# Making the attention's products on GpSimd, in chunks of 1024 elements

## The chip, the cores and the metric

The kernel runs on one core of a Trainium2 chip. The core has a matrix engine (TensorE, PE in the profile), a vector engine (VectorE, DVE), a scalar engine (ScalarE, ACT), a general engine (GpSimd, POOL) and a queue for transfers (SyncE, SP). Each engine carries out its own instructions in their order, and waits on semaphores for what other engines made. The metric is the device time of one launch in microseconds. The kernel before took 472.21 us, the median of three runs (471.46 to 473.74).

## The reference

The input x has shape (2, 1024, 256), in float32. Two branches work on the normalized x, and both results are added to x.

```
xn = layernorm(x)
out = x + attention(xn) + experts(xn)

attention: each row of 256 is 16 tokens of 16 numbers
  qkv = tok @ qkv_w                      # q, k, v of 16 each
  two branches of 8 channels; in each, windows of 8 tokens
    s = softmax(q k^T / sqrt(8))         # 8 x 8 in every window
    o = s @ v + depthwise 3x3 convolution of v
  tok + layernorm(concat(o) @ proj_w + proj_b) * ln_w + ln_b

experts: 16 experts of 176 hidden units, gated by a sigmoid router
  the two best of four groups, then the six best experts of a row
  sum of weight * (silu(x @ gate^T) * (x @ up^T)) @ down^T
  and one shared expert of twice that width, for every row
```

In the attention each window has 8 queries, 8 keys and 8 channels. The scores of a window are 512 products, summed by eights. The weighted values are another 512 products, also summed by eights.

## The kernel before, in words

The work starts with loading x, normalizing it and transposing it (`xnT`). The router's choice follows on VectorE, with the shared expert's products beside it on TensorE. The rows are then sorted so that rows with the same set of experts come together. From about 100 us on, the experts' products run over 16 tiles of 128 sorted rows.

The loop at L965 writes the main part in program order. One *unit* is two expert products: `up` (L823) makes gate and up products on TensorE (L827), ScalarE takes the silu (L829), and VectorE multiplies the two and the row's weight into `hms` (L830). One unit later `hidden` transposes that (L841, L843), and another unit later `finished` makes the down products (L853 for two experts of one tile, L861 for extras) and adds them up (L908, or L916 for extras). Sixteen tiles have three units each. 13 units of *extras*, for rows whose tile has more than six experts, come after the first four tiles. When a tile is complete, `added` (L920) issues an indirect transfer from GpSimd's queue that adds its rows to the output (L922). The first four tiles' additions wait for the extras. `sorted_tile` (L796) gathers a tile's rows with an indirect transfer from GpSimd's queue (L798), transposes them on TensorE (L802), and prepares the weights on VectorE (L805, L807, L809, L810).

Between the units the loop lays steps of the attention. Every step has a cost, and a step is laid whenever the costs so far fall behind the share of the units that are done. A planner then orders each engine's instructions by its own estimate of when they can start; the order within an engine can differ from the program's.

The attention runs over four pairs of image b and half h, called heads in this document. For each, `gather` copies the rows, `project` (L654) makes q, k and v with eight products on TensorE (L656) and copies them on ScalarE (L658 to L661) into `qk` and `v`. Then 16 positions of windows, n = 0 to 15, are worked through, NW = 4 at a time, so that one chunk is 4 x 8 x 8 x 8 = 2048 elements in each of 128 partitions:

- `products` (L665) multiplies q and k of the chunk, each broadcast (L669), and `scores` sums the last axis (L673). Both are VectorE's.
- `highest` takes the maximum (L679), subtracts it (L680), and ScalarE takes the exponential (L681).
- `weighted` (L687) multiplies s and v (L690), and `values` sums (L695). `totals` makes the denominators (L684, L685) after the first weighted chunk.
- `divide` (L703) multiplies by the reciprocals, and `transposed` turns the result on TensorE (L710) and copies it to `oT` (L712).

The chunk's products lie in a work tile with the tag "prod", of which there is one buffer; later the first of the two result tiles `att` takes the same tag. `qk` and `v` have one buffer each, so the next head's projections wait for the last products of this head.

After the fourth head, `attended` (L746) runs eight times: the output projection and the convolution on TensorE (L761), the second normalization on ScalarE and VectorE (L771 to L783). `attention_added` (L945) adds the result to the output with transfers from GpSimd's queue (L946).

Of the kernel before, what the change touches and what calls it, by code (L numbers as in the profile page):

```python
# [8 lines left out]
F32 = mybir.dt.float32  # L9
# [4 lines left out]
ALU = mybir.AluOpType  # L14
# [8 lines left out]
P = 128  # L23
B, H, W = 2, 1024, 256
C = 16
HD = 8
WIN = 8
NW = 4
E, I = 16, 176
LAST = I - P  # L30
HALF = P // 2
# [18 lines left out]
def csw_block_moe(ctx: ExitStack, tc: tile.TileContext, x, qkv_w, conv_w0, conv_b0, conv_w1, conv_b1,  # L50
# [19 lines left out]
    nc = tc.nc  # L70
# [3 lines left out]
    work = ctx.enter_context(tc.tile_pool(name="work", bufs=1))  # L74
# [69 lines left out]
    for c in range(16):  # L144
        n = sum(P // 2 if k % 2 == 0 else P for k in range(c)) + (((16 - c) * P - 1) / 2 if c % 2 == 0 else 0)
# [186 lines left out]
    full = [P, 16, E]  # L332
# [114 lines left out]
    for c in range(15, -1, -1):  # L447
        n = 16 - c
# [186 lines left out]

    oT = big.tile([P, 4, 2, 4, P], F32, name="oT", tag="oT")

    def attention(b, h):
        steps = []

        qk = work.tile([P, 2, 2, 8, WIN, HD], F32, tag="qk", name=f"qk{b}{h}")
        v = work.tile([P, 2, 8, HD, WIN], F32, tag="v", name=f"v{b}{h}")
        s = work.tile([P, 16, WIN, WIN], F32, tag="f1024", name=f"s{b}{h}", bufs=3)
        o = work.tile([P, 16, WIN, HD], F32, tag="f1024", name=f"o{b}{h}", bufs=3)
        sums = small.tile([P, 16, WIN], F32, name=f"sums{b}{h}", tag="sums")
        rows = work.tile([P, 8, P], F32, tag="f1024", name=f"rows{b}{h}", bufs=3)
        full = [P, NW, WIN, WIN, HD]

        def gather():
            for i in range(2):  # L650
                nc.scalar.copy(rows[:, 4 * i : 4 * i + 4].rearrange("p i (w r) -> p i w r", r=4),
                               xnT[:, h, :, 64 * b : 64 * b + 64].rearrange("p (i r) (w u) -> p u i w r", r=4, u=2)[:, i])

        def project(i):  # L654
            pq = ps_m.tile([P, 3, 8, C], F32, tag="m", name="pq")
            nc.tensor.matmul(pq.rearrange("p s t c -> p (s t c)"), lhsT=rows[:, i],  # L656
                             rhs=wq.rearrange("p s t c -> p (s t c)"), start=True, stop=True)
            nc.scalar.copy(qk[:, :, 0, i], pq[:, 0:2, :, 0:HD])  # L658
            nc.scalar.copy(qk[:, :, 1, :, i], pq[:, 0:2, :, HD:C])
            nc.scalar.copy(v[:, 0, i], pq[:, 2, :, 0:HD].rearrange("p t c -> p c t"))  # L660
            nc.scalar.copy(v[:, 1, :, :, i], pq[:, 2, :, HD:C])  # L661

        held = {}

        def products(n):  # L665
            pr = work.tile([P, NW, WIN, WIN, HD], F32, tag="prod", name="pr")
            br, m = n // 8, n % 8
            q_, k_ = (qk[:, part, br, m : m + NW] for part in range(2))
            nc.vector.tensor_tensor(pr, q_.unsqueeze(3).to_broadcast(full), k_.unsqueeze(2).to_broadcast(full), ALU.mult)  # L669
            held[n] = pr  # L670

        def scores(n):
            nc.vector.tensor_reduce(out=s[:, n : n + NW], in_=held.pop(n), axis=AX.X, op=ALU.add)  # L673

        rows_s = s.rearrange("p n q k -> p (n q) k")

        def highest():
            top = small.tile([P, P], F32, tag="top", name="top", bufs=1)
            nc.vector.tensor_reduce(out=top, in_=rows_s, axis=AX.X, op=ALU.max)  # L679
            nc.vector.tensor_tensor(rows_s, rows_s, top.unsqueeze(2).to_broadcast([P, P, WIN]), ALU.subtract)  # L680
            nc.scalar.activation(rows_s, rows_s, AF.Exp, scale=HD**-0.5)  # L681

        def totals():
            nc.vector.tensor_reduce(out=sums.rearrange("p n q -> p (n q)"), in_=rows_s, axis=AX.X, op=ALU.add)  # L684
            nc.vector.reciprocal(sums, sums)  # L685

        def weighted(n):  # L687
            pr = work.tile([P, NW, WIN, HD, WIN], F32, tag="prod", name="pv")
            br, m = n // 8, n % 8
            nc.vector.tensor_tensor(pr, s[:, n : n + NW].unsqueeze(3).to_broadcast(full),  # L690
                                    v[:, br, m : m + NW].unsqueeze(2).to_broadcast(full), ALU.mult)
            held[n] = pr

        def values(n):
            nc.vector.tensor_reduce(out=o[:, n : n + NW], in_=held.pop(n), axis=AX.X, op=ALU.add)  # L695

        def divide():
            xo = held["xo"] = work.tile([P, 8, 8, C], F32, tag="xo", name=f"xo{b}{h}")
            for br in range(2):
                to = xo[:, :, :, HD * br : HD * br + HD]  # L700
                if br:
                    to = to.rearrange("p i t c -> p t i c")
                nc.vector.tensor_tensor(to, o[:, 8 * br : 8 * br + 8],  # L703
                                        sums[:, 8 * br : 8 * br + 8, :].unsqueeze(3).to_broadcast([P, 8, WIN, HD]),
                                        ALU.mult)

        def transposed(i):
            po = ps_m.tile([P, 4, P], F32, tag="m", name="po")
            for j in range(4):
                nc.tensor.transpose(po[:, j, :], held["xo"][:, i + j].rearrange("p t c -> p (t c)"), ident)  # L710
            to = oT.rearrange("p g h r (b w i) -> p g h b i w r", b=B, i=2)[:, :, h, b, i // 4]
            nc.scalar.copy(to, po.rearrange("p j (w r) -> p j w r", r=4))  # L712


        steps.append((512, gather))
        for i in range(8):
            steps.append((512, lambda i=i: project(i)))
        for n in range(0, 16, NW):
            steps.append((2048, lambda n=n: products(n)))
            steps.append((2048, lambda n=n: scores(n)))  # L720
        steps.append((2048, highest))
        for n in range(0, 16, NW):
            steps.append((2048, lambda n=n: weighted(n)))
            if n == 0:
                steps.append((2048, totals))
            steps.append((2048, lambda n=n: values(n)))
        steps.append((1024, divide))
        for i in (0, 4):
            steps.append((512, lambda i=i: transposed(i)))
        return steps  # L730

    def edges():

        xe = [work.tile([P, 2, 4, P], F32, tag=tag, name="xe") for tag in ("v", "xo")]
        for t in xe:
            nc.gpsimd.memset(t, 0.0)
        pairs = xnT.rearrange("p h l (q e) -> p l h q e", e=2)
        for h in range(2):  # L740
            above, below = (t[:, h].rearrange("p l (q e) -> p l q e", e=2) for t in xe)
            nc.vector.tensor_copy(above[:, :, :, 1], pairs[:, 12:16, h, :, 0])
            nc.vector.tensor_copy(below[:, :, :, 0], pairs[:, 0:4, h, :, 1])
        return xe
# [181 lines left out]
    att = []  # L926

    def all_steps():
        for steps in (extras_listed(), weights_prepared()):
            for _ in steps:  # L930
                yield 1024, lambda: None
        yield from attention_steps()

    def attention_steps():
        for b in range(B):
            for h in range(2):
                yield from attention(b, h)
        xe = []
        yield 1024, lambda: xe.extend(edges())
        att.extend(work.tile([P, 8, W], F32, tag=tag, name="att") for tag in ("prod", "qk"))  # L940
        for g in range(4):
            for h in range(2):
                yield 3584, lambda: attended(g, h, xe, att)
# [122 lines left out]
```

## Time and profile before

| | |
|---|---|
| median of three runs | 472.21 us |
| the profiled execution | 474.59 us |
| its span | 472.9 us |
| TensorE busy | 414.2 us |
| VectorE busy | 324.6 us |
| ScalarE busy | 213.1 us |
| GpSimd busy | 72.7 us |
| VectorE in products (L669, L690) | 36.6 + 36.6 us |
| VectorE in sums (L673, L695) | 36.5 + 36.4 us |
| mean granted TensorE clock | 0.978 |

A row of a group gives the line, the engine, the operation, the output and input with partitions x elements, and the count; behind the first bar the busy time in us and the mean of one in ns; behind the second the engine's idle time before these instructions and what ended it. A row in order of time starts with the start and the duration in us; a bracket at its end gives the idle time before it and what ended that. "PEld" is TensorE loading weights, beside its products. TensorE's busy time is modelled at the ends and overlaps from one product to the next, so that a busy TensorE is not one at its peak.

### The profile page before, as it was taken

How to read it: one execution, taken by the hardware profiler on the slowest of the kernel's cores; microseconds unless marked ns; L12 is line 12 of the kernel's file. 1: busy time of each engine (PE TensorE's matmuls, PEld its weight loads, DVE VectorE, ACT ScalarE, POOL GpSimd, SP SyncE). 2: the span in 40 equal slices, each digit the busy share in tenths (PEclk: the TensorE clock that was granted, in tenths of full speed). 3: DMA queues.
4: the chain of work that ended last, by engine and by line, in shares of the span. 5: the costliest groups of instructions: out<-in, count | busy, mean ns of one | idle time of the engine just before them, and what ended most of it. 6: DMA issues, size and time to landing. Idle time of an engine off the chain costs nothing.

```text
span 472.9 us, 6428 instructions
## 1 busy us (share of the span) xinstructions
PE 414.2 (88%) x1726; PEld 258.7 (55%) x1727; DVE 324.6 (69%) x587; ACT 213.1 (45%) x510; POOL 72.7 (15%) x94
## 2 busy tenths in 40 slices
PE   0999999997989789999999998889989998999950
PEld 0446566464557566655566665546655555557740
DVE  4525956745789994997972799969999456665210
ACT  1946167222644537546425536263422566674210
POOL 6300000425530000000002301201111101002321
PEclk9999999997999999999999999999999999999995
DMA  8999950423120000000012211101231112104841
GB/s 225 325 291 272 285 163 2 101 47 79 57 58 28 21 21 19 22 19 28 24 30 42 43 36 36 35 16 31 44 71 30 14 54 67 54 14 74 124 77 15
DMA packets 37714, 35.39 MB, mean 75 GB/s; under 512 B 4000, under 2 KB 36112, under 8 KB 37648
## 3 DMA queue, kind: packets, MB, share of 16 engines
q1 hardware_dynamic: 30448, 25.37, 19.3%
q0 software_dynamic: 6176, 8.56, 11.6%
q10 hardware_dynamic: 1056, 1.05, 0.7%
q8 instruction: 16, 0.26, 0.2%
q14 instruction: 18, 0.15, 0.1%
HBM read 26.45 MB, written 10.62 MB: 78 GB/s over the span
## 4 chain that ended last, share of the span: by engine, by line
DVE 36%; PE 33%; DMA 13%; ACT 7%; issue 6%; POOL 1%; DVEq 1%; POOLq 0%; SPq 0%; ACTq 0%
PE pr_u L827 8%; DVE pv L690 6%; DVE o L695 6%; DVE s L673 5%; DVE pr L669 5%; DMA xg<-xw_d,of 5%; PE pp L761 4%; DVE hms L830 4%; DMA out_dram<-att 3%; PE pr_y L861 3%; PE pg L266 3%; DMA out_dram<-ysum,of 3%; PE py L281 2%; PE pq L656 2%; DMA xx<-in_x_dram 2%
## 5 line engine op out<-in xcount | busy, mean ns | idle before, releaser
L827 PE MATMUL pr_u<-w1s,xsT 128*128 x384 | 129.8, 469 | 5.2 <-DVE hms L830 5.0
L829 ACT ACTIVATE sg<-pr_u 128x176 f32<-128x176 f32 x122 | 38.3, 317 | 128.7 <-PE pr_u L827 98.2
L827 PEld LDWEIGHTS pr_u<-w1s,xsT 128*128 128x128 f32 x384 | 70.8, 191 | 42.5 <-DVE hms L830 10.5
L922 POOL DMA_INDIRECT out_dram<-ysum,of x16 | 27.0, 1691 | 246.8 <-DVE ysum L916 116.6
L830 DVE SCALAR_TENSOR_TENSOR hms<-sg,w,pr_u 128x176 f32<-128x176 f32 x96 | 36.9, 390 | 38.0 <-ACT sg L829 37.9
L669 DVE TENSOR_TENSOR pr<-qk 128x2048 f32<-128x2048 f32 x16 | 36.6, 2287 | 7.8 <-ACT qk L658 7.6
L841 PE MATMUL ph<-ident,hms 128*128 128x128 f32 x183 | 33.3, 279 | 6.9 <-DVE hms L830 5.4
L690 DVE TENSOR_TENSOR pv<-s,v 128x2048 f32<-128x2048 f32 x16 | 36.6, 2286 | 3.5 <-ACT s L681 3.5
L841 PEld LDWEIGHTS ph<-ident,hms 128*128 128x128 f32 x183 | 23.4, 142 | 26.3 <-DVE hms L830 11.3
L673 DVE TENSOR_REDUCE s<-pr 128x256 f32<-128x2048 f32 x16 | 36.5, 2279 | 0.0
L695 DVE TENSOR_REDUCE o<-pv 128x256 f32<-128x2048 f32 x16 | 36.4, 2272 | 0.0
L827 PE MATMUL pr_u<-w1s,xd 128*128 x104 | 33.5, 460 | 1.1 <-ACT xd L868 1.1
L843 ACT COPY hT<-ph 128x384 f32<-128x384 f32 x61 | 29.1, 478 | 3.3 <-PE ph L841 1.7
L853 PE MATMUL pr_y<-w2a,hT 128*128 x96 | 28.7, 381 | 0.0
L853 PE MATMUL pr_y<-w2b,hT 112*128 x96 | 28.7, 379 | 0.0
L853 PE MATMUL pr_y<-wts,hT 128*128 128x256 f32 x96 | 28.6, 379 | 0.0
L656 PE MATMUL pq<-wq,rows 128*128 128x384 f32 x64 | 25.0, 501 | 2.3 <-ACT oT L712 1.7
L827 PEld LDWEIGHTS pr_u<-w1s,xd 128*128 128x128 f32 x104 | 19.7, 190 | 11.0 <-ACT xd L868 1.5
L281 PE MATMUL py<-room 128*128 128x256 f32 x96 | 23.9, 387 | 1.4 <-DVE room L275 1.4
L266 PE MATMUL pg<-xnT,room 128*128 128x512 f32 x48 | 24.1, 614 | 0.0
L798 POOL DMA_INDIRECT xg<-xw_d,of x16 | 20.2, 1262 | 22.4 <-PE px__928 L802 8.6
L266 PE MATMUL pu<-xnT,room 128*128 128x512 f32 x48 | 23.0, 602 | 0.0
(314 smaller groups left out, 623.4 us busy)
## 6 DMA issues: line engine op xcount, KB each, us to landing
w1s<-in_w_dram SPq DMA_DIRECT2D x22, 256.0 KB, 5.5
wts<-in_w_dram SPq DMA_DIRECT2D x61, 64.0 KB, 2.1
wts<-in_w_dram SPq DMA_DIRECT2D x61, 48.0 KB, 1.7
xw_d<-xx SPq DMA_DIRECT2D x4, 544.0 KB, 8.2
w2a<-in_w_dram SPq DMA_DIRECT2D x4, 512.0 KB, 11.5
out_dram<-ysh POOLq DMA_DIRECT2D x4, 512.0 KB, 5.5
xr<-xw_d SPq DMA_DIRECT2D x4, 512.0 KB, 3.8
out_dram<-att POOLq DMA_DIRECT2D x4, 512.0 KB, 7.2
```

What stands on the lines that cost most here:

```text
L266: nc.tensor.matmul(ps, lhsT=w1h[:, half, h, P * m : P * m + P], rhs=xnT[:, h, 4 * k : 4 * k + 4, :].rearrange("p l q -> p (l q)"), start=( ...
L281: nc.tensor.matmul(py, lhsT=hms[k, m][:, P * c : P * c + P], rhs=w2h[:, m], start=(m == 0), stop=(m == 2))
L656: nc.tensor.matmul(pq.rearrange("p s t c -> p (s t c)"), lhsT=rows[:, i], rhs=wq.rearrange("p s t c -> p (s t c)"), start=True, stop=True)
L669: nc.vector.tensor_tensor(pr, q_.unsqueeze(3).to_broadcast(full), k_.unsqueeze(2).to_broadcast(full), ALU.mult)
L673: nc.vector.tensor_reduce(out=s[:, n : n + NW], in_=held.pop(n), axis=AX.X, op=ALU.add)
L690: nc.vector.tensor_tensor(pr, s[:, n : n + NW].unsqueeze(3).to_broadcast(full), v[:, br, m : m + NW].unsqueeze(2).to_broadcast(full), ALU. ...
L695: nc.vector.tensor_reduce(out=o[:, n : n + NW], in_=held.pop(n), axis=AX.X, op=ALU.add)
L827: nc.tensor.matmul(pu, lhsT=lhs[:, h, :], rhs=w1s[:, :, h, bass.ds(e * I, I)], start=(h == 0), stop=(h == 1))
L829: nc.scalar.activation(sg, pu[:, 0, :], AF.Silu)
L830: nc.vector.scalar_tensor_tensor(hm[:, 0:I], sg, w, pu[:, 1, :], op0=ALU.mult, op1=ALU.mult)
L841: nc.tensor.transpose(ph[:, s, :], units[:, P * s : P * s + P], ident)
L853: nc.tensor.matmul(py, lhsT=l_, rhs=r_, start=start and n == 0, stop=stop and n == 2)
```

## The change

A chunk has two positions (1024 elements) instead of four. The product tile is made once, with room for two chunks, and chunks take the halves in turn; all four heads and the later `att` tile use it. The products are issued on GpSimd instead of VectorE, with the same operands. The sums stay on VectorE. The steps are laid so that a product comes one chunk ahead of the sum: product 0, product 1, sum 0, product 2, sum 1, and so on. The denominators (`totals`) come before the first weighted chunk instead of after it. A step of a product or sum costs 1024 instead of 2048, so a head's steps cost the same in all.

```diff
-NW = 4
+NW = 2
...
+    prods_ = []
+
     def attention(b, h):
         steps = []
+        if not prods_:
+            prods_.append(work.tile([P, 2, NW, WIN, WIN, HD], F32, tag="prod", name="prods"))
+        prods = prods_[0]
...
         def products(n):
-            pr = work.tile([P, NW, WIN, WIN, HD], F32, tag="prod", name="pr")
+            pr = prods[:, n // NW % 2]
             br, m = n // 8, n % 8
             q_, k_ = (qk[:, part, br, m : m + NW] for part in range(2))
-            nc.vector.tensor_tensor(pr, q_.unsqueeze(3).to_broadcast(full), k_.unsqueeze(2).to_broadcast(full), ALU.mult)
+            nc.gpsimd.tensor_tensor(pr, q_.unsqueeze(3).to_broadcast(full), k_.unsqueeze(2).to_broadcast(full), ALU.mult)
             held[n] = pr
...
         def weighted(n):
-            pr = work.tile([P, NW, WIN, HD, WIN], F32, tag="prod", name="pv")
+            pr = prods[:, n // NW % 2]
             br, m = n // 8, n % 8
-            nc.vector.tensor_tensor(pr, s[:, n : n + NW].unsqueeze(3).to_broadcast(full),
+            nc.gpsimd.tensor_tensor(pr, s[:, n : n + NW].unsqueeze(3).to_broadcast(full),
                                     v[:, br, m : m + NW].unsqueeze(2).to_broadcast(full), ALU.mult)
...
-        for n in range(0, 16, NW):
-            steps.append((2048, lambda n=n: products(n)))
-            steps.append((2048, lambda n=n: scores(n)))
+        def in_turn(product, total):
+
+            for n in range(0, 16 + NW, NW):
+                if n < 16:
+                    steps.append((1024, lambda n=n: product(n)))
+                if n >= NW:
+                    steps.append((1024, lambda n=n: total(n - NW)))
+
+        in_turn(products, scores)
         steps.append((2048, highest))
-        for n in range(0, 16, NW):
-            steps.append((2048, lambda n=n: weighted(n)))
-            if n == 0:
-                steps.append((2048, totals))
-            steps.append((2048, lambda n=n: values(n)))
+        steps.append((2048, totals))
+        in_turn(weighted, values)
...
-        att.extend(work.tile([P, 8, W], F32, tag=tag, name="att") for tag in ("prod", "qk"))
+        att.extend([prods_[0].rearrange("p a w q k d -> p (a w q k d)").rearrange("p (n d) -> p n d", d=W),
+                                       work.tile([P, 8, W], F32, tag="qk", name="att")])
```

## The prediction

> **What bounds the kernel now.** I read the busy shares, then the chain that ended last, then the costliest groups, and then the order in time of VectorE, GpSimd and TensorE around the attention.
>
> ```profile
> PE 414.2 (88%) x1726; PEld 258.7 (55%) x1727; DVE 324.6 (69%) x587; ACT 213.1 (45%) x510; POOL 72.7 (15%) x94
> ...
> DVE 36%; PE 33%; DMA 13%; ACT 7%; issue 6%; POOL 1%; DVEq 1%; POOLq 0%; SPq 0%; ACTq 0%
> ...
> L669 DVE TENSOR_TENSOR pr<-qk 128x2048 f32<-128x2048 f32 x16 | 36.6, 2287 | 7.8 <-ACT qk L658 7.6
> ...
> L690 DVE TENSOR_TENSOR pv<-s,v 128x2048 f32<-128x2048 f32 x16 | 36.6, 2286 | 3.5 <-ACT s L681 3.5
> ...
> L673 DVE TENSOR_REDUCE s<-pr 128x256 f32<-128x2048 f32 x16 | 36.5, 2279 | 0.0
> L695 DVE TENSOR_REDUCE o<-pv 128x256 f32<-128x2048 f32 x16 | 36.4, 2272 | 0.0
> ```
>
> GpSimd is nearly idle, and the chain is shared between VectorE and TensorE. The page does not say where, so I went to time. I call one (b, h) pair a head. From a head's first product to the end of its last division VectorE took 125.3 to 177.0 us, 183.6 to 244.8, 262.9 to 310.7 and 316.5 to 364.6. In heads 1, 3 and 4 the chain is VectorE nearly without a gap: 51.7, 47.8 and 48.1 us. In head 2 it is mostly TensorE, because the extra units run beside it. After 364.6 it is TensorE again, up to 455.9, and 17 us of output transfers end the span.
>
> How much work TensorE really has, I take from its undisturbed rhythm near the end:
>
> ```profile
> 440.42 2.53 PE L827 MATMUL pr_u<-w1s,xsT 128*128 x8
> ...
> 444.42 2.53 PE L827 MATMUL pr_u<-w1s,xsT 128*128 x8
> ```
>
> A unit (two expert products, their transposes, their down products) costs 4.0 us. By the built order there lie beside heads 1, 2, 3, 4 and behind them 21, 31, 21, 19 and 26 expert products. With projections and transposes that is 45 to 47 us of TensorE work in each of the 54 to 56 us from first projection to last transposition of heads 1, 3 and 4. So TensorE idles some 25 us there, waiting for gated products (L830) that stand behind 2.28 us attention operations on VectorE. That is all a faster VectorE could win.
>
> **Price of a chunk.** VectorE loses 32 products: 36.6 + 36.6 = 73.2 us. The 32 sums of 2048 become 64 of 1024. L679 is the same reduction of 1024 elements by eights, at 1.21 us, so 64 x 1.21 = 77.4 against 72.9. VectorE falls from 324.6 to about 256 us. GpSimd gains 64 two-input products. No row of before shows one. Its nearest rows are these:
>
> ```profile
> 2.31 0.30 POOL masks.py:199 TENSOR_SCALAR_AFFINE_SELECT ident<-ident 128x128 f32<-128x128 f32 x1
> ...
> 3.94 0.53 POOL L163 TENSOR_SCALAR_AFFINE_SELECT room<-room 128x256 f32<-128x256 f32 x1
> ...
> 365.77 0.95 POOL L738 MEMSET xe<- 128x1024 f32 x1 [3.84 <-PE po L710]
> ```
>
> A write alone is 0.95 us for 1024. One input and one output cost 0.23 us for 128 more elements, so 0.07 + 8 x 0.23 = 1.9 us for 1024, an estimate. This is the lower end, for a product has two inputs. Here the Trainium skill speaks against the change: "GPSIMD Engine Reference", section "Performance versus the Vector engine", gives 4497 ns for a two-input operation on 2048 fp32 elements, about twice VectorE's. (It gives 2293 for VectorE, and L669 shows 2287 here.) Half of it, with the 0.1 us fixed part of the memset rows, is 2.3 us for 1024, again an estimate. No run here shows it. I take 2.3, plus 0.05 for handing over, with 1.9 and 3.0 as ends, the upper one for patterns that run in pieces of eight elements.
>
> The two halves do double the buffer: in the built order a product waits for the sum two chunks back, and the first two of a head wait for ScalarE alone. So the period is GpSimd's 2.3, with VectorE's 1.21 and one or two L830 (0.39 each) beneath it. VectorE's own pace before was (2.287 + 2.279) / 2 = 2.28 for the same 1024. **GpSimd merely takes VectorE's place at the same pace.**
>
> **A head on GpSimd.** 16 x 2.3 = 36.8. Added to it is what cannot overlap: the last score sum 1.2, maximum 1.2, subtraction 1.2, one L830 0.4, exponential 1.1, last value sum 1.2, division 1.3, and 0.2 of handovers: 7.8. In all 44.6 us, against 47.8 to 51.7. What VectorE did between (L830, denominators, L908) is now hidden under GpSimd: 3 to 7 us won per head. Then comes what shares GpSimd's in-order queue.
>
> *Head 1.* Two projections instead of four suffice for the first product, so it starts near 123.0 instead of 125.3. Four row gathers (L798) now stand between products: 4 x (1.0 + 0.3) = 5.2. TensorE's transposes of those rows come up to 4 us later; the 9 us it idles here cover that, and without cover it would be 4 us more. Second rule: in "SBUF — State Buffer", section "Who interferes with whom", a VectorE instruction with two SBUF inputs and a GpSimd instruction that reads SBUF exclude each other for a whole instruction. Two rows agree that something of the kind exists:
>
> ```profile
> 121.04 0.95 POOL L798 DMA_INDIRECT xg<-xw_d,of x1 [0.30 <-DVE wsrt L805]
> ...
> 125.40 2.99 POOL L798 DMA_INDIRECT xg<-xw_d,of x1 [3.41 <-DVE wf L807]
> ```
>
> The second ran into the product at 125.29 (2.28 us) and took 2.04 us more, and so did 300.08 (3.36 instead of 1.56). Turned round, VectorE would wait for a product. Sums have one input, L830 reads one operand from PSUM, and the subtraction finds GpSimd idle, so only the small L805, L807 and L809 of head 1 are hit, about eight. By the rule they cost up to 8 x 1.2 = 9 us of VectorE time, of which most fits in its gaps; by the bare rows nothing. I take 2. Head 1 ends at 123.0 + 44.6 + 5.2 + 2 = 174.8, against 177.0: -2.2.
>
> *To the last extra (250.8 before).* TensorE binds. One unit that lay beside head 1 now lies here (33 products against 31): +4.0. The stretches at 183 to 207 and 230 to 236, where 2.28 us operations held L830 back, get about 3 back. End near 249.5: -1.3.
>
> *Head 3.* Four output additions (L922), all waiting for the last extra, now stand ahead of its first product. Each waits for the one before to land:
>
> ```profile
> 251.60 1.65 POOL L922 DMA_INDIRECT out_dram<-ysum,of x1 [116.62 <-DVE ysum L916]
> 256.29 1.58 POOL L922 DMA_INDIRECT out_dram<-ysum,of x1 [3.04 <-ACT sg L829]
> 260.60 1.55 POOL L922 DMA_INDIRECT out_dram<-ysum,of x1 [2.73 <-ACT sg L829]
> 265.36 1.56 POOL L922 DMA_INDIRECT out_dram<-ysum,of x1 [3.21 <-ACT v L661]
> ```
>
> That is 0.8 + 13.8 + 1.6 = 16.2 after the last extra, so the first product starts at 265.7 instead of 262.9. Before, these waits cost nothing; now the products wait, VectorE's first sum waits for them, and the L830 behind it and TensorE wait for that. Two more additions lie inside (2 x 1.55). End: 265.7 + 44.6 + 3.1 = 313.4, against 310.7: +2.7.
>
> *Head 4.* The third later addition stands ahead of its first product and needs a tile that is summed only after head 3's division and two more L830: about 6.2 us until the product, where 5.7 went before. The next addition stands behind the second product and waits for second sum, L830 and L908: 2.3 of stall and 1.6 of issue; one more costs 1.6. End: 313.4 + 6.2 + 44.6 + 5.5 = 369.7, against 364.6: +5.1.
>
> *The rest.* TensorE binds, with one unit more (28 products against 26): +4.0, so +9.1. Tail as before. The 0.05 of handover on 48 chunks adds 2.4. **Sum: +11.5 us** on a profiled execution of 474.6 (span 472.9, 1.7 around it). That execution lies 2.4 above the median shown, which moves with it: 472.2 + 11.5, rounded to 484 us. The three GpSimd-bound heads have 48 chunks, so each 0.1 us in a chunk's price moves the time by 4.8.
>
> **Rivals.** *A slower product* (chance 0.19). At 3.0 us: 0.7 x 48 = 34 more, 517; head 2 stays under TensorE. For it: pieces of eight with broadcast strides. Against it: the page's figure has no such piece.
>
> *A faster product* (0.15), the other side: one mechanism, GpSimd's rate, in heads 1, 3 and 4. At 1.9 us: -19, about 466; below that TensorE's 44 us beside each head binds. It decides at about 2.05, where the sum is even. For it: the one-input rows. Against it: those have one input.
>
> *No change to measure* (0.06): a product near 2.05, within 0.5% of 472.2 (about what a measurement of this kernel can tell from no change), 470 to 474.5.
>
> *The halves don't overlap*: product and sum in turn, 3.6 us, would give about 546. The waits in the build exclude it, so it has no chance of its own.
>
> **How the numbers follow.** My forecast has 0.60, with 475 to 500 as its own range: a chunk between 2.2 and 2.6. Slower by over 0.5% is 0.60 + 0.19 = 0.79, same 0.06, faster 0.15. The range is 468 to 510: a chunk from 2.0 to 2.85, leaving about 0.1 at either side.
>
> **What would show it.** The new rows for products: about 2.3 us, start to start, in heads 3 and 4. VectorE near 256 us busy, GpSimd near 220. VectorE's sums waiting for GpSimd, and TensorE's waits on L830 no smaller in heads 3 and 4. The first product of head 3 some 16 us after the last extra, and head 4's division ending near 370. I am wrong if a product is under 2.05 us; if VectorE's or TensorE's order holds GpSimd back, so that its spacing exceeds its duration; or if the small VectorE operations in head 1 wait far longer than 2 us in all.

## The result, and the profile after

The changed kernel took 514.56 us, the median of four runs (512.22 to 515.9), beside 472.73 us for the kernel before (the median of four runs; the 472.21 us above is that of the first three): a ratio of 1.088 (95% interval 1.083 to 1.093). It is 42 us slower. I had forecast 484 us and a range of 468 to 510: the right direction, a size of about a quarter, and a range that ends too early.

The page of the changed kernel, with the lines that answer to those shown of before (the profiled execution took 515.9 us):

```profile
span 514.2 us, 6502 instructions
...
PE 424.9 (83%) x1726; PEld 265.1 (52%) x1727; DVE 273.7 (53%) x587; ACT 213.4 (42%) x510; POOL 215.9 (42%) x158
...
PE 36%; POOL 24%; DVE 15%; DMA 11%; issue 6%; ACT 5%; DVEq 0%; POOLq 0%; SPq 0%; ACTq 0%
...
L674 POOL TENSOR_TENSOR prods<-qk 128x1024 f32<-128x1024 f32 x32 | 76.0, 2595 | 33.9 <-ACT qk L663 30.4
L695 POOL TENSOR_TENSOR prods<-s,v 128x1024 f32<-128x1024 f32 x32 | 75.2, 2514 | 21.2 <-ACT s L686 21.2
...
L678 DVE TENSOR_REDUCE s<-prods 128x128 f32<-128x1024 f32 x32 | 38.9, 1218 | 45.2 <-POOL prods L674 45.2
L700 DVE TENSOR_REDUCE o<-prods 128x128 f32<-128x1024 f32 x32 | 38.9, 1215 | 25.1 <-POOL prods L695 24.9
```

GpSimd has VectorE's place in the chain, 24% of the span. VectorE's sums now wait 70 us for GpSimd. No engine is busier than before in any way that would explain 42 us: TensorE shows 11 us more, with ends that are modelled, and VectorE 51 us less. So the time is in waits. The mean granted clock was 0.960, beside 0.978 before, but it was lower than before only inside the four heads (0.93 to 0.97, before 1.00). In the stretches below that grew most it was 1.00 wherever no head was running, so the clock is not what made them longer. Lines of the code after this point are those of the changed kernel: L838 is what L830 was, the gated product; L930 what L922 was, the output addition.

The waits of TensorE from 120 us on, first before and then after (engine and what it was to do, what it waited for, us in all, times, longest):

```profile
PE ph L841 <- DVE hms L830: 5.4, 9, 0.9
PE pr_u L827 <- DVE hms L830: 5.0, 5, 1.9
```

```profile
PE pr_u L835 <- DVE hms L838: 19.5, 11, 4.0
PE ph L849 <- DVE hms L838: 18.8, 13, 4.8
```

TensorE's waits for gated products went from 10.4 to 38.3 us. That is where most of the 42 us are, and the question is why VectorE, with less to do, hands them over later.

I cut both executions at the same places, the ones that the prediction's sum names. "Head" is from the first product to the end of the last division:

| stretch, us | before | predicted | after |
|---|---|---|---|
| start to end of head 1 | 177.0 | 174.8 | 176.4 |
| to the last extra's addition | 73.8 | 74.7 | 90.5 |
| to the first product of head 3 | 12.1 | 16.2 | 13.4 |
| head 3 | 47.8 | 47.7 | 48.9 |
| to the first product of head 4 | 5.7 | 6.2 | 13.4 |
| head 4 | 48.1 | 50.1 | 50.5 |
| to the last tile's sum | 91.3 | 95.3 | 103.2 |
| transfers at the end | 17.0 | 17.0 | 17.9 |
| span | 472.8 | 482.0 | 514.2 |

(The forecast's 2.4 us for handovers are in no row.)

Heads 1, 3 and 4 lasted as predicted, within about 1.5 us each. The excess of 31 us lies in three stretches in which TensorE is at work: 15.8, 7.2 and 7.9. The first of them holds head 2, which the prediction had left to TensorE. Head 2 itself fell from 61.2 to 48.0 us, now as long as GpSimd needs. But the gap ahead of it grew from 6.6 to 14.0 us, and the stretch from its end to the last extra's addition from 6.0 to 28.5 us, and TensorE was busy in nearly all of both. In heads 1, 3 and 4 TensorE was busy for 110.5 of 152.4 us, before for 131.4 of 147.6. So work of TensorE has moved out of the heads.

TensorE between the end of head 3 (VectorE's last division ends at 329.2) and the projections of head 4, in order of time:

```profile
329.65 2.53 PE L835 MATMUL pr_u<-w1s,xsT 128*128 x8
...
333.65 2.53 PE L835 MATMUL pr_u<-w1s,xsT 128*128 x8
...
337.65 1.04 PE L715 MATMUL po<-ident,xo 128*128 128x128 f32 x8
339.38 0.91 PE L661 MATMUL pq<-wq,rows 128*128 128x384 f32 x2 [0.69 <-ACT oT L717]
```

Before, the same transposition (L710, now L715) came right after the division:

```profile
310.78 1.09 PE L710 MATMUL po<-ident,xo 128*128 128x128 f32 x8 [1.69 <-DVE xo L703]
```

After, two units stand ahead of the transposition in TensorE's queue, 8 us. They could have been done beside the head, where TensorE had little to do, but gated products that they wait for stand behind the head's last sums on VectorE. After heads 1, 3 and 4 the transposition starts 7.3, 8.4 and 7.1 us after the last division ends, before the change 0.1 us after it. I then counted, in the built order of VectorE's queue, how many of its 123 gated products (one of them in a last loop that isn't entered here) stand between a head's first sum (or product, before) and its last division:

| | head 1 | head 2 | head 3 | head 4 | outside |
|---|---|---|---|---|---|
| before | 18 | 24 | 17 | 16 | 48 |
| after | 12 | 14 | 13 | 12 | 72 |

The head's length is given by GpSimd whatever stands in it. A gated product outside costs TensorE's 2 us per expert product in series. 24 x 2 = 48 us more outside, less 8.5 us by which the four heads together were shorter, is 40 us. That was the theory to test.

### The profile page after: what moved, and what is told of

It reads as the page before. It is cut to its first block, busy times and chain, and to the rows that moved or that the text cites. A ratio compares the mean times of both kernels' runs of the same rounds, so it can differ in the third digit from the quotient of the medians.

```text
span 514.2 us, 6502 instructions
## 1 busy us (share of the span) xinstructions
PE 424.9 (83%) x1726; PEld 265.1 (52%) x1727; DVE 273.7 (53%) x587; ACT 213.4 (42%) x510; POOL 215.9 (42%) x158
## 4 chain that ended last, share of the span: by engine, by line
PE 36%; POOL 24%; DVE 15%; DMA 11%; issue 6%; ACT 5%; DVEq 0%; POOLq 0%; SPq 0%; ACTq 0%
POOL prods L695 12%; PE pr_u L835 10%; POOL prods L674 9%; PE pp L769 5%; PE pr_y L861 4%; DMA out_dram<-ysum,of 4%; PE pr_y L869 2%; PE pg L266 2%; DMA xg<-xw_d,of 2%; DMA out_dram<-att 2%; PE py L281 2%; DVE wsrt L813 2%; DMA xx<-in_x_dram 2%; DVE s L678 2%; POOL out_dram L930 2%
## 5 line engine op out<-in xcount | busy, mean ns | idle before, releaser
L835 PE MATMUL pr_u<-w1s,xsT 128*128 x384 | 133.6, 475 | 19.7 <-DVE hms L838 19.5
L674 POOL TENSOR_TENSOR prods<-qk 128x1024 f32<-128x1024 f32 x32 | 76.0, 2595 | 33.9 <-ACT qk L663 30.4
L695 POOL TENSOR_TENSOR prods<-s,v 128x1024 f32<-128x1024 f32 x32 | 75.2, 2514 | 21.2 <-ACT s L686 21.2
L930 POOL DMA_INDIRECT out_dram<-ysum,of x16 | 25.2, 1578 | 101.3 <-DVE ysum L916 38.3
L838 DVE SCALAR_TENSOR_TENSOR hms<-sg,w,pr_u 128x176 f32<-128x176 f32 x96 | 36.9, 391 | 52.1 <-ACT sg L837 52.0
L678 DVE TENSOR_REDUCE s<-prods 128x128 f32<-128x1024 f32 x32 | 38.9, 1218 | 45.2 <-POOL prods L674 45.2
L700 DVE TENSOR_REDUCE o<-prods 128x128 f32<-128x1024 f32 x32 | 38.9, 1215 | 25.1 <-POOL prods L695 24.9
L849 PE MATMUL ph<-ident,hms 128*128 128x128 f32 x183 | 35.0, 290 | 18.8 <-DVE hms L838 18.8
L284 POOL DMA_DIRECT2D out_dram<-ysh x4 | 3.7, 936 | 65.0 <-ACT ysh L282 65.0
L861 PE MATMUL pr_y<-w2a,hT 128*128 x96 | 30.5, 402 | 0.0
L661 PE MATMUL pq<-wq,rows 128*128 128x384 f32 x64 | 24.5, 497 | 2.0 <-ACT oT L717 1.2
L835 PEld LDWEIGHTS pr_u<-w1s,xd 128*128 128x128 f32 x104 | 19.5, 190 | 12.1 <-ACT xd L876 2.6
L806 POOL DMA_INDIRECT xg<-xw_d,of x16 | 16.6, 1039 | 17.7 <-PE px__928 L810 8.5
```

The costliest lines, as they stand in the source:

```text
L674: nc.gpsimd.tensor_tensor(pr, q_.unsqueeze(3).to_broadcast(full), k_.unsqueeze(2).to_broadcast(full), ALU.mult)
L695: nc.gpsimd.tensor_tensor(pr, s[:, n : n + NW].unsqueeze(3).to_broadcast(full), v[:, br, m : m + NW].unsqueeze(2).to_broadcast(full), ALU. ...
L835: nc.tensor.matmul(pu, lhsT=lhs[:, h, :], rhs=w1s[:, :, h, bass.ds(e * I, I)], start=(h == 0), stop=(h == 1))
L838: nc.vector.scalar_tensor_tensor(hm[:, 0:I], sg, w, pu[:, 1, :], op0=ALU.mult, op1=ALU.mult)
L849: nc.tensor.transpose(ph[:, s, :], units[:, P * s : P * s + P], ident)
L861: nc.tensor.matmul(py, lhsT=l_, rhs=r_, start=start and n == 0, stop=stop and n == 2)
```

## The experiments

**Is the length of a head GpSimd's?** Each product makes only the first of its two windows. The other half is set to zero once and summed as it is, so this kernel leaves out half of the attention's products. The instruction order hardly changes (73 gated products outside the heads instead of 72).

```diff
-            nc.gpsimd.tensor_tensor(pr, q_.unsqueeze(3).to_broadcast(full), ...
+            nc.gpsimd.tensor_tensor(pr[:, 0:1], q_[:, 0:1].unsqueeze(3).to_broadcast(part_), ...
...                                   # the weighted products in the same way; a memset of the tile, once, is left out here
```

> The changed kernel with each GpSimd product making only the first of its two windows (512 elements; the other half of the room is set to zero once and summed as it is): that part of the attention is left out. 73 gated products stand outside the heads, as in the changed kernel (72), so the layout is the same and only GpSimd's time changes. If GpSimd's rate sets the length of a head (49 to 53 us now), heads fall to what VectorE needs, about 33 us plus the output additions, 34 to 38: 4 x 14 less, 452 to 468, with the gaps between the heads as long as now. If heads were held up by something else (exclusion, handovers, TensorE), little moves: 500 to 512.

Measured 464.1 us. The product took 1.27 us instead of 2.36 (shortest, median and longest in ns, first the changed kernel):

```profile
L674 POOL TENSOR_TENSOR prods<-qk x32: 2336/2361/2942, 123.4 to 361.9; 128x1024 f32<-128x1024 f32 x32
```

```profile
L676 POOL TENSOR_TENSOR prods<-qk x32: 1255/1270/1850, 121.4 to 318.0; 128x512 f32<-128x512 f32 x32
```

Heads lasted 36.9, 41.3, 33.7 and 36.1 us instead of 53.0, 48.0, 48.9 and 50.5, in all 52 us less. Each stretch between and behind them stayed within 2.1 us of what it was. So GpSimd's rate does set the heads, and 1.09 us per product moved the time by 50 us, 4.6 us for each 0.1. That this is near the prediction's 4.8 is in part chance: the prediction counted 48 chunks in three heads, here 64 chunks in four heads were shortened, and each head by less than its chunks, because at 1.27 us GpSimd comes to wait for VectorE's sums of 1.21 us in places (7.7 us in the weighted products). The run also shows that the gaps are not set by that rate.

**Does the layout cost, with GpSimd left out?** Two kernels with the products on VectorE, in chunks of 2048 as before. In both, the attention's products and sums and the gated products are pinned to program order. They differ in the steps' costs alone, and so in how many units are laid beside a head (50 gated products outside the heads in the first, 71 in the second).

```diff
 # both, here one of five places
+            tc.keep_in_program_order(nc.vector.tensor_reduce(out=s[:, n : n + NW], in_=held.pop(n), axis=AX.X, op=ALU.add))
 # the second only
-            steps.append((2048, lambda n=n: products(n)))       # scores, weighted, values too
+            steps.append((1400, lambda n=n: products(n)))
-            steps.append((512, lambda i=i: project(i)))         # gather, divide, transposed too
+            steps.append((1418, lambda i=i: project(i)))
```

> Control: the kernel before with VectorE's attention products, sums and gated products pinned to program order. 50 gated products outside the heads, as in the kernel before (49). Both theories: 469 to 478.

> The same as the control, but with the steps' costs set so that fewer gated products are laid beside a head: 71 stand outside the heads, nearly as many as in the changed kernel (72). All products stay on VectorE in chunks of 2048. Theory 1: 21 x 2 us more outside, against some 11 from a shorter head 2 and 6 from 15 fewer gated products in VectorE's heads: about +23, 490 to 500. Theory 2: no GpSimd products, so like the control, under 480.

Measured 487.0 and 507.6 us. The control missed: pinning alone costs 13 us. Head 1 begins at 130.3 us instead of 125.3, and the gaps ahead of heads 2 and 4 are 5.7 and 3.0 us longer. So only the difference between the two counts. It is 20.6 us, where 23 had been worked out. In their profiles the heads together are 22.5 us shorter and the stretches ahead of them 42.4 us longer, 9.0 of it ahead of head 1. A loss of this kind needs no GpSimd product: the layout is enough for it.

**Is it the chunks, or the order of the steps?** All of the change, with the products on VectorE.

```diff
-            nc.gpsimd.tensor_tensor(pr, q_.unsqueeze(3)...
+            nc.vector.tensor_tensor(pr, q_.unsqueeze(3)...
```

> The change with its chunks, its halves and its step order, but with the products on VectorE. 44 gated products outside the heads (49 in the kernel before). Theory 1: five fewer outside save 10 us, 128 operations of 1024 instead of 64 of 2048 cost 9: 470 to 477. Theory 2: also near the kernel before, as GpSimd makes no products. A time over 485 would say that chunking itself costs.

Measured 471.5 us, beside 474.1 for the kernel before on the same chip: a ratio of 0.994 (0.992 to 0.997). Halved chunks, two halves and the new step order cost nothing. This was the fastest version that makes all of the products, by half a percent.

**A first repair of the order.** The change with its sums pinned to program order.

```diff
-            nc.vector.tensor_reduce(out=s[:, n : n + NW], in_=held.pop(n), axis=AX.X, op=ALU.add)
+            tc.keep_in_program_order(nc.vector.tensor_reduce(out=s[:, n : n + NW], in_=held.pop(n), axis=AX.X, op=ALU.add))
```

> The change, with VectorE's sums of the products pinned behind everything written before them in program order, so that the planner can't move them ahead of gated products. In the built order 72 of VectorE's 123 gated products stand outside the heads in the changed kernel, here 52. Theory 1 (layout: every gated product outside the heads costs 2 us of TensorE time in series, since heads last as long as GpSimd needs): 20 x 2 us less, and head 2 longer by about 10 because TensorE binds it: 484 us (478 to 490). Theory 2 (the products on GpSimd hold VectorE and TensorE back by exclusion and handovers, whatever the order): 505 to 515.

Measured 498.2 us: 16 us less, where 30 were expected. It fits neither theory. Head 2 took 75.8 us instead of 48.0, with 30 gated products in it, from its first product to its last division, instead of 14. I had put that at 10 us; it was 27.8. Pinning also costs of itself, as the control showed. A better repair had to copy an order that is known to run well.

**The order alone, and the additions alone.** Three kernels. In the first, each of the 64 sums is put behind as many gated products as stand ahead of it in the run with all chunks on VectorE. In the second, the output additions are laid and pinned behind GpSimd's last product. The third has both.

```diff
 # first and third: AHEAD is read from the built order of the run with chunks on VectorE
+    def in_place(ins):
+        ahead = hs_[: AHEAD[len(sums_)]]
+        sums_.append(ins)
+        if ahead:
+            tc.add_manual_dep(ins.ins, ahead[-1].ins.name, ...)      # order only, no wait
...
-        nc.vector.scalar_tensor_tensor(hm[:, 0:I], sg, w, ...
+        hs_.append(nc.vector.scalar_tensor_tensor(hm[:, 0:I], sg, w, ...   # the list of gated products
-            nc.vector.tensor_reduce(out=s[:, n : n + NW], in_=held.pop(n), axis=AX.X, op=ALU.add)
+            in_place(nc.vector.tensor_reduce(out=s[:, n : n + NW], in_=held.pop(n), axis=AX.X, op=ALU.add))   # values too
 # second and third
-        nc.gpsimd.indirect_dma_start(out=out_rows, ...
+        tc.keep_in_program_order(nc.gpsimd.indirect_dma_start(out=out_rows, ...
-            for t in ready[:1]:
+            for t in ready[:1] if walked >= 4 * 43520 + 11 * 1024 else []:
```

> The change with each of VectorE's 64 sums put behind as many gated products as stand ahead of it in the run with all chunks on VectorE (471.5 us); the products stay on GpSimd. 46 gated products outside the heads instead of 72 (44 in that run). Theory 1 (layout): 26 x 2 us leave the gaps; head 2, which takes 11 more extras' products, becomes bound by TensorE and grows by some 20; the others grow by 1 to 5: 478 to 492. What remains above 471.5 is then the price of GpSimd itself. Theory 2 (exclusion and handovers whatever the order): above 500.

> The changed kernel with the output additions laid and pinned behind the last of GpSimd's products. In the built order none stands among the products any more. 72 gated products outside the heads, as now. Theory 1: head 3 starts up to 6 us earlier and heads 3 and 4 lose six issues: 502 to 511. Rival (the additions hold the products back and are the main loss): 480 to 495.

> Both edits together: VectorE's order as in the run with all chunks on VectorE, and the additions behind the products. If the two causes add up: the first run's time less what the second saves, 470 to 488. Under 471.5 it would be the faster of the two ways to split the chunks.

| | us | against 514.6 |
|---|---|---|
| order | 490.1 | -24.5 |
| additions behind | 501.2 | -13.4 |
| both | 476.5 | -38.0 |
| the kernel before, beside these runs | 473.6 | |

The two add up: 24.5 + 13.4 = 37.9, and both together give 38.0. That is closer than these figures are known (each median stands for runs that lie 2 to 4 us apart, and the kernel before took 0.9 us more beside these runs than beside the changed kernel). That GpSimd's products hold VectorE and TensorE back whatever the order ("theory 2", above 500 us) is excluded: in the first and the third GpSimd still makes every product.

In the first, TensorE's waits for gated products from 120 us on are below what they were before the change (6.9 against 10.4 us), and the transpositions after heads 1, 3 and 4 follow the division by 0.1 us again. What TensorE waits for more than before is the division itself, as heads 1, 3 and 4 are up to 4.3 us longer than before the change: 12.3 us, before 2.1.

```profile
PE po L725 <- DVE xo L718: 12.3, 3, 5.1
PE pr_u L845 <- DVE hms L848: 4.3, 3, 1.9
...
PE ph L859 <- DVE hms L848: 2.6, 3, 1.4
```

The second saves at the places that were named: ahead of head 3 (36.5 us from head 2's end, 41.9 before that edit), in head 3 (46.7 against 48.9) and in head 4 (46.3 against 50.5). Its 501.2 us lie 0.8 us under the range expected. The rival, that the additions are the main part, falls: they are a third. What is left of both, 476.5 against 473.6 (ratio 1.006, 1.004 to 1.007), is small, and products on GpSimd bring nothing. It is no clean price of theirs: against the run with all chunks on VectorE, whose order was copied, the difference is 5 us (with the additions at other places), and in the gaps after heads 1 and 3, which are 1.5 and 1.8 us longer than before the change, the granted clock was 0.79 and 0.56, before 1.00. This was not taken apart further.

An earlier try at the additions laid them later without pinning them. 

> The changed kernel with all output additions laid after the fourth head, so that none stands among GpSimd's products. 72 gated products outside the heads, as now. Theory 1 (layout): only the lead of head 3 (some 5 us) and six issues and one stall (8 us) go, 500 to 506. Rival (GpSimd's queue: the additions and what they wait for hold the products back and are the main part of the loss): 480 to 492.

Measured 513.1 us, which decides nothing: the planner had put the additions back where they were, and the order of GpSimd's queue was that of the changed kernel.

**A part of the chunks on GpSimd.** Every second or every fourth product.

```diff
-            nc.gpsimd.tensor_tensor(pr, ...
+            (nc.gpsimd if n // NW % 2 else nc.vector).tensor_tensor(pr, ...       # second run: n // NW % 4 == 1
```

> The change, but only every second chunk's product on GpSimd, the others on VectorE. GpSimd needs 8 x 2.3 us in a head, VectorE about 43 in all. 60 gated products outside the heads. Heads of 44 to 47 us instead of 48 to 53 and 12 fewer outside: 514 - 4 x 5 - 24 = 470 (464 to 480). If two-input VectorE products and GpSimd products shut each other out and handovers cost on top, 480 to 490.

> Only every fourth chunk's product on GpSimd. 49 gated products outside the heads, as in the kernel before. VectorE loses 4 x 1.14 us in a head against the run with all chunks on VectorE (471.5): 471.5 - 3 x 4 = 460 (456 to 466) where heads are bound by VectorE; with exclusion as long as a GpSimd product (2.3 us) four times a head, no gain: 468 to 474.

Measured 495.7 and 490.3 us: both expectations missed. Sharing the products doesn't shorten a head: 51.8 to 56.8 us in the first, 51.8 to 56.5 in the second. VectorE's own products, 1.22 us when GpSimd is quiet, run into GpSimd's. The instructions on the product tile in the run with every second chunk (shortest, median and longest duration in ns):

```profile
L674 DVE TENSOR_TENSOR prods<-qk x16: 1211/1226/3708, 121.8 to 348.4; 128x1024 f32<-128x1024 f32 x16
...
L695 DVE TENSOR_TENSOR prods<-s,v x16: 1210/2006/3690, 151.1 to 374.2; 128x1024 f32<-128x1024 f32 x16
```

In the run with every fourth chunk the layout is nearly that of before (49 outside). There the additions act inside head 3. Its first product is VectorE's, at 263.66, and waits only for the projections. GpSimd's first product stands behind the four output additions, and VectorE's second sum waits 6.27 us for it:

```profile
269.75 2.93 POOL L674 TENSOR_TENSOR prods<-qk 128x1024 f32<-128x1024 f32 x1
...
272.71 1.22 DVE L678 TENSOR_REDUCE s<-prods 128x128 f32<-128x1024 f32 x1 [6.27 <-POOL prods L674]
```

So one product of a head behind the output additions is enough to hold the head. That these two effects make up the whole of both misses was not tested.

## Why the prediction was wrong, point by point

*The price of a chunk was right.* The 2.3 us were an estimate worked out from a figure of the Trainium skill ("GPSIMD Engine Reference", "Performance versus the Vector engine"). The eight weighted products of head 1 follow each other at 18.50 / 8 = 2.31 us:

```profile
155.46 18.50 POOL L695 TENSOR_TENSOR prods<-s,v 128x1024 f32<-128x1024 f32 x8 [5.12 <-ACT s L686]
```

The page states 4497 ns for a two-input operation on 2048 elements, half of which is 2.25 us, and the trace agrees; pieces of eight elements with broadcast strides did not make it slower here. The group's mean of 2595 ns is longer because the rows that follow an output addition, up to 2.94 us long, overlap the one before; they too start 2.3 us apart. The step "GpSimd merely takes VectorE's place at the same pace" holds too. GpSimd's busy time was 215.9 us (220 forecast). The sign that would have spoken against it, VectorE's order holding GpSimd back, showed only in head 1, where two products waited 3.5 us for sums.

*The length of a head was right within about 2 us*, including what cannot overlap: heads 3 and 4 took 46.7 and 46.3 us without the additions, 44.6 forecast.

*The additions in GpSimd's queue were right.* I had 4.1 us for the lead of head 3 and 3.1 and 5.5 for those inside the heads, in all 12.7. Taking them out gave 13.4.

*The exclusion was seen, and was larger than allowed for.* VectorE and GpSimd in head 1, in order of time:

```profile
122.65 0.18 DVE L813 COPY wsrt<-xg 128x16 f32<-128x16 f32 x1 [0.94 <-DMA xg<-xw_d,of]
...
123.84 1.98 DVE L813 COPY wsrt<-xg 128x16 f32<-128x16 f32 x1 [0.73 <-DMA xg<-xw_d,of]
...
140.78 4.74 DVE L813 COPY wsrt<-xg 128x16 f32<-128x16 f32 x2
```

```profile
123.45 4.75 POOL L674 TENSOR_TENSOR prods<-qk 128x1024 f32<-128x1024 f32 x2 [1.42 <-ACT qk L663]
...
140.76 4.64 POOL L674 TENSOR_TENSOR prods<-qk 128x1024 f32<-128x1024 f32 x2
```

The copy of sixteen elements at 123.84 ends at 125.82, as GpSimd's first product does (125.80). The row at 140.78 holds two copies. The first took 4.67 us and ended at 145.44, as the second of two products in a row does (145.40); the other then took 0.16 us. The rule as the prediction tells it is for two inputs in SBUF; this copy has one and waited all the same. L813 and L817 took 10.9 us more than before in all (up to 9 in the prediction), which is most of why VectorE's busy time was 273.7 and not 256. So the prediction's last sign of being wrong, waits far longer than 2 us in all, did show. It is not where the time went: head 1 ended 1.6 us later than forecast, with 2 us allowed for the waits. How much of the 10.9 us reached that end was not measured.

*The step that failed* is this: "By the built order there lie beside heads 1, 2, 3, 4 and behind them 21, 31, 21, 19 and 26 expert products", and the two lines that rest on it, "One unit that lay beside head 1 now lies here (33 products against 31): +4.0" and "with one unit more (28 products against 26): +4.0". I counted on TensorE's queue, from the first projection to the last transposition, and took what lies there as work that a head hides. But a transposition stands behind the division, and TensorE can't get far ahead of the gated products. What a head hides is what VectorE's queue has between the head's first sum and its last division: 12, 14, 13 and 12 products instead of the 19, 33, 19 and 19 that TensorE's queue has there. The rest stood in TensorE's queue ahead of the transposition and behind late gated products, and was done in series: 7 to 8 us after each of heads 1, 3 and 4, and ten products more stood behind head 2, where the stretch grew by 22.5 us. In the sum I had 8 us for the whole of it (two units), less 3 that a freer VectorE would win back. The three stretches took 31 us more than forecast, and mending VectorE's order alone took 24.5 back, which is what shows the cause. The other 6 were not separated.

*The direction.* The additions were 12.7 of the forecast 11.5 us, and came true. The other terms nearly cancelled in the sum, and did not in the run. So the mechanism behind the right direction is a third of the loss.

*The rivals.* "A slower product" would have given 517 and so looks right by its number, but its mechanism is not there: the product took 2.3 us. My range was made from the product's price alone. It had no case in which the order of VectorE's queue takes work out of the heads, and that is why it ended at 510.

*What stays open:* why the planner laid fewer gated products between the sums. With products of half the size it laid as few (73 outside), so the size of a product does not explain it. It goes with the share of the products that GpSimd makes: 44 stand outside with none of them there, 49 with every fourth, 60 with every second and 72 with all. How the planner comes to this was not looked into.

## What to carry to other kernels

When work moves to another engine and an automatic planner orders the queues, read the built order of every in-order queue that the moved work waits in or makes others wait in, and count what stands between its first and its last instruction there: work counted on the engine that does it (TensorE here) is not hidden if its inputs stand behind the moved work's consumers (VectorE's sums). Transfers that wait for something late and share GpSimd's queue become a wait for the compute that is put behind them. Half-size products on VectorE with a double buffer, without GpSimd, were the version to keep, by half a percent.

## What the runs showed of the hardware that I had not expected

- A 128x16 fp32 copy on VectorE, 0.18 us by itself, took 1.98 us, and another 4.67 us, while GpSimd made 128x1024 two-input products. The first ended when GpSimd's product did, the second only after two products in a row.
- A VectorE product of 128x1024 (1.21 us) took up to 3.71 us beside GpSimd's products. The two runs that shared the products between the engines took 495.7 and 490.3 us, beside 471.5 with all of them on VectorE.
- GpSimd's two-input product took 1.27 us for 512 elements and 2.36 us for 1024: by these two sizes, 2.13 ns for an element of a partition and 0.18 us fixed. VectorE's sums of the same tile ran beside it at their usual 1.22 us.
